# A graph layer's dense product by Strassen's scheme: seven quarter products for eight, summed in stages

## The chip, the core and the metric

The kernel runs on one NeuronCore of a Trainium2 chip. A core has five engines that issue their instructions in program order and meet at semaphores: PE (TensorE, matrix products into PSUM), DVE (VectorE), ACT (ScalarE), POOL (GpSimd) and SP, which here only starts DMA transfers. [...] The metric is the time of one execution on the device in microseconds.

## What is computed

The input `x` holds 32 batches of 512 nodes by 1024 columns, `adj` is a 512 x 512 matrix.

```
# layer 0, for each batch b
q = wq . x[b];  k = wk . x[b]                       # 1024 each
scores[m, n] = leaky_relu(q[n] + k[m], 0.01)
att = softmax(scores, axis=-1)                      # 1024 x 1024
agg = x[b] @ att.T;  y = relu(adj @ agg + bm)
x[b] = layernorm(x[b] + y)                          # over the 1024 columns
# layer 1
W = adj * adj                                       # element by element
x[b] = layernorm(x[b] + W.T @ x[b] + bias)
```

## The kernel before

**Layer 0** never forms the attention matrix. For leaky_relu the softmax weight of a pair is a product of two exponentials, one pair of them on each side of zero. So for a batch the kernel forms q and k (`pa`, `pc`, `co`, `cc`, `ro`, `rc`), finds by comparison the rank of each column among the q (`rk` on DVE) and how many q lie above the threshold of each row (`ct` on ACT), computes z = adj @ x in eight row tiles of 128 x 512 (`z`, 32 matmul calls; `zc` copies each from PSUM into the SBUF tile `zt`), scatters the rows of z in order of rank to HBM (`sc`, an indirect DMA on POOL's queue), loads them back sorted (`sl`), takes exponentials (`se`), running sums in both directions (`u`, `d`), carries across partitions (`cu`, `uc`, `cd`, `dc`), finished sums (`tu`, `td`, `te`), and writes them as a table (`tw`, `tl`). A gather (`g`, indirect DMA) fetches for each row its two table entries; `mw`, `ms`, `mx` weigh and add them, `t` transposes them on PE, `r` adds x and applies the relu, `s0` sums squares, `rt` and `rce` make the reciprocal of the deviation.

**Layer 1** is one product of a 512 x 512 matrix with the batch's 512 x 1024. `adj_2` is adj squared by element plus the identity, so the residual is inside the product. `scaled` (`w`, line 460, DVE) multiplies its four row tiles by the batch's reciprocal deviations instead of scaling x. `layer1` (`l`, line 469, PE) makes output row tile m, half h, with four matmul calls of 128 x 512 over the row tiles n; both halves share a PSUM tile of two banks. `biased` (`b`, line 480, DVE) adds the bias, held as a 128 x 1024 tile, writes the row tile `g` to SBUF and sums it; `s1` (ACT) sums squares, `r1` (POOL) makes deviation and shift, `n` (line 497, ACT) normalises in place and `st` (SP) stores. The mean of layer 0's norm is never subtracted: a constant along a row of x becomes a constant along the rows of the output, and the last norm takes that out.

**Order.** Nothing is scheduled by the machine. Three lists of words (`head`, `loop`, `tail`) are written out by hand and `emit` issues them in that order; a word such as `l.-4.2.0` is an operation, a batch relative to the loop's and its tile. Each engine gets its own instructions in the order of the list, so batches overlap: in one pass of `loop` the z of one batch, the running sums of the batch before and the layer 1 of the batch before that go by together. Waits come from data: a reader waits for its writer, and a buffer's next writer waits for its last reader. PSUM is two pools: `p1`, four tiles of one bank (tag `m`: z, carries, q and k), and `p2`, two tiles of two banks (tag `w`: transposes, layer 1). `zt`, `tab`, `got` and the scaled weights have one buffer, x has four, `g` four.

Of the kernel before, what the change touches and what calls it, by code (L numbers as in the profile page):

```python
# [24 lines left out]
F32 = mybir.dt.float32  # L26
# [7 lines left out]
P = 128  # L34
# [6 lines left out]
def adj_resnorm_kernel(  # L41
# [42 lines left out]
    rows = one.tile([P, CT, C], F32, tag="w2", name="rows")[0 : 3 * CT, 0, 0:P]  # L84
# [6 lines left out]
    bias_b = const.tile([P, N], F32, name="bias_b")  # L91
# [39 lines left out]
    adj_2 = const.tile([P, CT, C], F32, name="adj_2")  # L131

    def weights():
# [12 lines left out]
        for r in range(CT):  # L146
            a, own = adj_2[:, r, :], adj_2[:, r, r * P : (r + 1) * P]
            nc.gpsimd.tensor_tensor(a, adj_in[:, r, :], adj_in[:, r, :], ALU.mult)
            nc.gpsimd.tensor_tensor(own, own, ident, ALU.add)

# [6 lines left out]
    class Batch:  # L157
        def __init__(self):
            self.z, self.agg, self.l1, self.g = {}, {}, {}, {}
            self.w, self.v0, self.v1 = None, [], []  # L160
# [295 lines left out]
    def scaled(b, n):  # L456
        s = st[b]
        if n == 0:
            s.w2 = one.tile([P, CT, C], F32, tag="w2", name=f"w2_{b}")
        nc.vector.tensor_scalar(s.w2[:, n, :], adj_2[:, n, :], s.v0[1][:, n : n + 1], None, ALU.mult)  # L460


    def layer1(b, m, h):
        s, t = st[b], xts[b]
        if h == 0:
            s.l1[m] = p2.tile([P, N], F32, tag="w", name=f"l1_ps_{b}_{m}")
        at = slice(h * H, (h + 1) * H)
        for n in range(CT):
            nc.tensor.matmul(  # L469
                s.l1[m][:, at], s.w2[:, n, m * P : (m + 1) * P], t[:, n, at],  # L470
                start=(n == 0), stop=(n == CT - 1),
            )

    def biased(b, m):
        s = st[b]
        if not s.v1:
            s.v1 = stats(b, "1")
            s.nb = sp.tile([P, CT], F32, tag="nb", name=f"nb_{b}")
        s.g[m] = op.tile([P, N], F32, tag="g", name=f"g_{b}_{m}")
        nc.vector.scalar_tensor_tensor(  # L480
            s.g[m], s.l1[m], 1.0, bias_b, ALU.mult, ALU.add, accum_out=s.v1[0][:, m : m + 1]
        )
# [21 lines left out]
    def load_bias(b):  # L504
        nc.sync.dma_start(out=bias_b, in_=bias.partition_broadcast(P))

# [11 lines left out]
        "w": scaled, "l": layer1, "b": biased, "s1": spread1, "r1": root1, "n": norm1,  # L518
        "st": store, "bias": load_bias,
# [12 lines left out]
    ld.1 ld.2 pa.0 z.0.1 pc.0 co.0 zc.0.1 pa.1 cc.0 z.0.6 ro.0 z.0.0 rc.0 rk.0.0 ct.0.3 ct.0.4  # L532
    rk.0.3 z.0.2 ct.0.7 rk.0.2 pc.1 oq.0 ct.0.2 rk.0.5 z.0.3 zc.0.0 rk.0.1 zc.0.2 zc.0.6 rk.0.6
    rk.0.7 z.0.4 zc.0.3 ct.0.6 rk.0.4 re.0 sc.0.0 co.1 zc.0.4 z.0.5 cc.1 ct.0.5 sc.0.6 ct.0.1
    sc.0.2 sc.0.4 ro.1 zc.0.5 ct.0.0 sc.0.1 z.0.7 ce.0 sc.0.5 rc.1 we.0 sc.0.3 rk.1.3 z.1.3
    zc.0.7 ct.1.4 sc.0.7 rk.1.4 rk.1.1 z.1.0 rk.1.2 sl.0.0 rk.1.5 sl.0.1 ld.3 oq.1 rk.1.7 z.1.6
    rk.1.6 rk.1.0 se.0.0 z.1.1 ct.1.7 u.0.0 u.0.1 zc.1.3 u.0.2 se.0.1 zc.1.6 u.0.3 zc.1.0 pa.2
    u.0.4 u.0.5 z.1.7 pc.2 re.1 ct.1.5 u.0.6 u.0.7 ct.1.1 d.0.7 ct.1.2 d.0.6 z.1.4 d.0.5 zc.1.1
    ct.1.3 d.0.4 zc.1.7 d.0.3 ct.1.6 cu.0 d.0.2 pa.3 uc.0 d.0.1 zc.1.4 tu.0.0 sc.1.4 co.2 z.1.2
    pc.3 ct.1.0 cc.2 sc.1.3 tu.0.1 sc.1.6 d.0.0 sc.1.7 co.3 zc.1.2 ro.2 te.0 sc.1.2 cc.3 cd.0  # L540
    rc.2 sc.1.1 ro.3 dc.0 ce.1 ct.2.0 z.1.5 td.0.0 sc.1.0 ct.2.3 rk.2.5 tw.0.0 z.2.7 td.0.1
    zc.1.5 ct.2.1 sc.1.5 ct.2.7 rk.2.3 tw.0.1 bias.0 ct.2.5 z.2.0 tl.0 rk.2.4 ct.2.2 rk.2.7
    ct.2.6 rk.2.6 z.2.1 ct.2.4 rk.2.1 zc.2.0 zc.2.7 rk.2.0 z.2.5 rk.2.2 oq.2 rc.3 sl.1.0 sl.1.1
# [220 lines left out]
```

## Time and profile before

| | |
|---|---|
| median of 3 runs | 2082.99 us (2082.99 to 2087.58) |
| the profiled execution | 2081.17 us, its span 2079.4 us |
| PE busy | 2042.6 us, 98% |
| DVE busy | 1609.8 us, 77% |
| ACT busy | 1234.2 us, 59% |
| POOL busy | 881.8 us, 42% |
| HBM read and written | 270.80 MB and 269.29 MB, 260 GB/s |
| products of layer 1 (line 469) | 2048 instructions, 898.3 us |
| products z (line 260) | 2048 instructions, 912.4 us |

A group of the profile is read so: line of the kernel, engine, operation, output and inputs by name, shapes, count; then the busy time of the group and the mean duration of one instruction in ns; then the time that the engine stood idle just before, and what ended it. An fp32 matmul call shows as two instructions. Durations of neighbours overlap a little, so the step from one start to the next is shorter than the mean duration.

### The profile page before, as it was taken

How to read it: one execution, taken by the hardware profiler on the slowest of the kernel's cores; microseconds unless marked ns; L12 is line 12 of the kernel's file. 1: busy time of each engine (PE TensorE's matmuls, PEld its weight loads, DVE VectorE, ACT ScalarE, POOL GpSimd, SP SyncE). 2: the span in 40 equal slices, each digit the busy share in tenths (PEclk: the TensorE clock that was granted, in tenths of full speed). 3: DMA queues.
4: the chain of work that ended last, by engine and by line, in shares of the span. 5: the costliest groups of instructions: out<-in, count | busy, mean ns of one | idle time of the engine just before them, and what ended most of it. 6: DMA issues, size and time to landing. Idle time of an engine off the chain costs nothing. (4 is left out here: it accounts for less than half of the span.)

```text
span 2079.4 us, 21612 instructions
## 1 busy us (share of the span) xinstructions
PE 2042.6 (98%) x6737; PEld 1000.6 (48%) x6737; DVE 1609.8 (77%) x2700; ACT 1234.2 (59%) x2112; POOL 881.8 (42%) x1083
## 2 busy tenths in 40 slices
PE   8999999999999999999999999999999999999986
PEld 4444554445445445444445454455454445444443
DVE  4879879777788777788777887777887778777762
ACT  3646666655665556665556655557655567554554
POOL 3343454435434345344354343454443441444441
PEclk9999999999999999999999999999999999999998
DMA  4667776768676677676686666776766865676752
GB/s 187 262 268 301 272 296 266 271 261 320 235 276 238 254 299 284 243 271 236 264 324 248 265 248 251 286 299 236 279 232 257 320 254 238 228 299 269 284 213 81
DMA packets 138095, 541.53 MB, mean 260 GB/s; under 512 B 14414, under 2 KB 14426, under 8 KB 129788
## 3 DMA queue, kind: packets, MB, share of 16 engines
q1 hardware_dynamic: 80608, 337.99, 42.1%
q0 software_dynamic: 57344, 202.15, 25.5%
q8 instruction: 53, 0.87, 0.2%
q14 instruction: 62, 0.51, 0.1%
q10 hardware_dynamic: 28, 0.01, 0.0%
HBM read 270.80 MB, written 269.29 MB: 260 GB/s over the span
## 5 line engine op out<-in xcount | busy, mean ns | idle before, releaser
L260 PE MATMUL z_ps<-adj_t,x 128*128 128x512 f32 x2048 | 912.4, 595 | 3.4 <-ACT zt L266 3.4
L469 PE MATMUL l_ps<-x,w 128*128 128x512 f32 x2048 | 898.3, 595 | 8.8 <-DVE w L460 7.6
L469 PEld LDWEIGHTS l_ps<-x,w 128*128 128x128 f32 x2048 | 390.0, 191 | 500.6 <-issue 477.3
L260 PEld LDWEIGHTS z_ps<-adj_t,x 128*128 128x128 f32 x2048 | 380.4, 190 | 438.8 <-issue 428.9
L274 POOL DMA_INDIRECT sorted_z<-zt,to x256 | 356.4, 1392 | 465.7 <-ACT zt L266 304.6
L234 ACT ACTIVATE junk_s<-qb,qkc 128x1024 bf16<-128x1024 f32 x256 | 293.5, 1146 | 104.0 <-DVE qb L211 99.9
L382 POOL DMA_INDIRECT got<-table,of x256 | 275.9, 1078 | 160.8 <-issue 75.0
L221 DVE SCALAR_TENSOR_TENSOR junk_v<-qb,qkc,tie 128x1024 uint8<-128x1024 f32 x256 | 328.3, 1282 | 5.8
L404 ACT ACTIVATE got<-got,w 128x512 f32<-128x512 f32 x256 | 168.7, 712 | 238.5 <-DVE w L399 222.1
L425 POOL TENSOR_SCALAR var<-var 128x1 f32<-128x1 f32 x128 | 37.6, 294 | 535.4 <-ACT junk L418 530.8
L266 ACT COPY zt<-z_ps 128x512 f32<-128x512 f32 x256 | 146.3, 576 | 191.5 <-PE z_ps L260 188.7
L480 DVE SCALAR_TENSOR_TENSOR g<-l_ps,bias_b 128x1024 f32<-128x1024 f32 x128 | 156.2, 1221 | 92.0 <-PE l_ps L469 70.9
L409 DVE SCALAR_TENSOR_TENSOR got<-got,w 128x512 f32<-128x512 f32 x256 | 181.7, 747 | 24.1 <-ACT got L404 18.8
L418 ACT ACTIVATE junk<-g,tot 128x1024 bf16<-128x1024 f32 x128 | 146.8, 1147 | 48.4 <-DVE g L480 43.0
L322 DVE SCALAR_TENSOR_TENSOR tab<-tab,ac 128x513 f32<-128x513 f32 x224 | 168.2, 751 | 4.6
L440 DVE SCALAR_TENSOR_TENSOR x<-agg_ps,nbm,x 128x1024 f32<-128x1024 f32 x128 | 163.0, 1280 | 11.1 <-PE agg_ps L432 9.6
L497 ACT ACTIVATE g<-g,nb,var 128x1024 f32<-128x1024 f32 x128 | 158.4, 1244 | 10.6 <-POOL nb L491 10.6
L418 ACT ACTIVATE junk<-x,tot 128x1024 bf16<-128x1024 f32 x128 | 147.0, 1149 | 16.2 <-DVE x L440 11.3
L312 DVE SCALAR_TENSOR_TENSOR tab<-tab,ac 128x514 f32<-128x514 f32 x192 | 144.3, 751 | 15.3 <-ACT ac L298 12.4
L355 DVE TENSOR_TENSOR tab<-tab,carry 128x2052 f32<-128x2052 f32 x64 | 146.7, 2293 | 2.7 <-ACT carry L337 0.7
L432 PEld LDWEIGHTS agg_ps<-ident,got 128*128 128x128 f32 x1024 | 117.8, 141 | 54.2 <-issue 39.7
L432 PE MATMUL agg_ps<-ident,got 128*128 128x128 f32 x1024 | 133.0, 274 | 5.5 <-DVE g L480 2.3
(79 smaller groups left out, 1247.1 us busy)
## 6 DMA issues: line engine op xcount, KB each, us to landing
table<-tab SPq DMA_DIRECT2D x64, 2056.0 KB
tab<-sorted_z SPq DMA_DIRECT2D x64, 1028.0 KB
x<-in_x_dram SPq DMA_DIRECT2D x128, 512.0 KB
out_dram<-g SPq DMA_DIRECT2D x128, 512.0 KB
sorted_z<-zt,to POOLq DMA_INDIRECT x256
got<-table,of POOLq DMA_INDIRECT x256
adj_in<-in_adj_dram SPq DMA_DIRECT2D x1, 1024.0 KB
bias_b<-in_L_gnn_bias_dram SPq DMA_DIRECT2D x1, 512.0 KB
```

The source lines that it names most:

```text
L221: nc.vector.scalar_tensor_tensor(junk, s.qb, s.q[:, j : j + 1], tie[:, at : at + N], ALU.subtract, ALU.is_gt, accum_out=s.rank[:, j : j + 1],)
L234: nc.scalar.activation(junk, s.qb, AF.Sign, bias=s.k[:, j : j + 1], accum_out=s.sign[:, j : j + 1])
L260: nc.tensor.matmul(s.z[j], xt[:, c, j * P : (j + 1) * P], adj_t[:, c, :], start=(c == 0), stop=(c == CT - 1),)
L274: nc.gpsimd.indirect_dma_start(out=sorted_z[b % 2][:, :], out_offset=bass.IndirectOffsetOnAxis(ap=s.to[:, j : j + 1], axis=0), in_=zt[:, j ...
L322: nc.vector.scalar_tensor_tensor(v, v, c, s.zs[:, j + 1, 0:D], ALU.mult, ALU.add)
L382: nc.gpsimd.indirect_dma_start(out=s.got[:, j, :], out_offset=None, in_=table[b % 2][:, :], in_offset=bass.IndirectOffsetOnAxis(ap=s.of[:, ...
L404: nc.scalar.activation(down, down, AF.Copy, scale=s.w[:, 1, j : j + 1])
L409: nc.vector.scalar_tensor_tensor(up, up, s.w[:, 0, j : j + 1], down, ALU.mult, ALU.add)
L418: nc.scalar.activation(junk, t, AF.Square, bias=v[0][:, i : i + 1], scale=-float(N), accum_out=v[1][:, i : i + 1],)
L432: nc.tensor.transpose(s.agg[o][:, j * P : (j + 1) * P], s.got[:, j, o * P : (o + 1) * P], ident)
L440: nc.vector.scalar_tensor_tensor(t[:, o, :], s.agg[o], nbm[:, o : o + 1], t[:, o, :], ALU.max, ALU.add, accum_out=s.v0[0][:, o : o + 1],)
L469: nc.tensor.matmul(s.l1[m][:, at], s.w2[:, n, m * P : (m + 1) * P], t[:, n, at], start=(n == 0), stop=(n == CT - 1),)
```

## The change

Layer 1's product is cut into 2 x 2 quarters: the matrix into A11, A12, A21, A22 of 256 x 256, the batch into X11 to X22 of 256 x 512. Eight quarter products become seven (Winograd's form of Strassen's scheme), with

```
S1 = A21 + A22   S2 = S1 - A11   S3 = A11 - A21   S4 = A12 - S2
T1 = X12 - X11   T2 = X22 - T1   T3 = T2 - X11    T4 = T2 - X21
U  = A11 X11                      C11 = U + A12 X21
V  = U + S2 T2                    C12 = V + S1 T1 + S4 X22
Y  = V + S3 T3                    C21 = Y - A22 T4
                                  C22 = Y + S1 T1
```

- The S are made once, on POOL in `weights`. x must now be scaled before the T are formed: `norm0` (`n0`, ACT) scales its four row tiles in place, and `scaled` is gone. The T are made on DVE for each batch: T1 over X12 in place, T2 in a tile of its own, T3 and T4 in rows of `zt`.
- Each quarter product is made for two row tiles g = 0, 1 (two calls of 128 x 512 each). U, V and Y pile up in one PSUM bank (`sum`, from `p1`), and ACT copies U and then V out of it between the stages (`Uc`, `Vc`) into the row tile `g`. A12 X21 and S1 T1 (+ S4 X22) go to the two banks of `pair` (from `p2`); `Zc` copies S1 T1 out before `12` adds to it. `up` (DVE) adds pair to the copies of U and V for the upper row tiles; `lr` (DVE) adds Y to the copy of S1 T1; then `21` adds the last product onto Y and `ll` (ACT) copies it out; `ls` adds the two part sums.
- The bias comes in through PE: it is split into three bf16 parts for each half, six rows in all (`bias_parts`, once, on DVE), and a bf16 product with six rows of constants opens U (bias of the left half) and Z (difference of the halves).
- The `head`, `loop` and `tail` lists are new throughout; the loop is run for batches 11 to 24 instead of 10 to 26.

```diff
+        A21, A22 = S1, minus_A22
+        nc.gpsimd.tensor_tensor(S3, A11, A21, ALU.subtract)
+        nc.gpsimd.tensor_tensor(S1, A21, A22, ALU.add)
+        nc.gpsimd.tensor_tensor(S2, S1, A11, ALU.subtract)
+        nc.gpsimd.tensor_tensor(S4, A12, S2, ALU.subtract)
+        nc.gpsimd.tensor_scalar(minus_A22, A22, -1.0, None, ALU.mult)
...
-    def scaled(b, n):
-        s = st[b]
-        if n == 0:
-            s.w2 = one.tile([P, CT, C], F32, tag="w2", name=f"w2_{b}")
-        nc.vector.tensor_scalar(s.w2[:, n, :], adj_2[:, n, :], s.v0[1][:, n : n + 1], None, ALU.mult)
+    def norm0(b, o):
+        t = xts[b][:, o, :]
+        nc.scalar.activation(t, t, AF.Copy, scale=st[b].v0[1][:, o : o + 1])
+    def T1(b):
+        X11, X12, _, _ = quarters(b)
+        st[b].T1 = X12
+        nc.vector.tensor_tensor(X12, X12, X11, ALU.subtract)
+    def T2(b):
+        s = st[b]
+        s.T2 = one.tile([P, 2, H], F32, tag="T2", name=f"T2_{b}")
+        nc.vector.tensor_tensor(s.T2, quarters(b)[3], s.T1, ALU.subtract)
+    def T3(b):
+        st[b].T3 = zt[:, 0:2, 0:H]
+        nc.vector.tensor_tensor(st[b].T3, st[b].T2, quarters(b)[0], ALU.subtract)
+    def T4(b):
+        st[b].T4 = zt[:, 2:4, 0:H]
+        nc.vector.tensor_tensor(st[b].T4, st[b].T2, quarters(b)[2], ALU.subtract)
+    def quarter(ps, a, v, g, first=None):
+        if first is not None:
+            nc.tensor.matmul(ps, first, bias_p, start=True, stop=False)
+        for k in range(2):
             nc.tensor.matmul(
-                s.l1[m][:, at], s.w2[:, n, m * P : (m + 1) * P], t[:, n, at],
-                start=(n == 0), stop=(n == CT - 1),
+                ps, a[:, k, g * P : (g + 1) * P], v[:, k, :], start=False, stop=(k == 1),
+                skip_group_check=first is None,
             )
+    def U(b, g):
+        s = st[b]
+        s.sum[g] = p1.tile([P, C], F32, tag="m", name=f"sum_ps_{b}_{g}")
+        quarter(s.sum[g], A11, quarters(b)[0], g, first_0)
+    def U_copy(b, g):
+        rows1(b, g)
+        nc.scalar.copy(st[b].g[g][:, 0:H], st[b].sum[g])
+    def V(b, g):
+        quarter(st[b].sum[g], S2, st[b].T2, g)
+    def V_copy(b, g):
+        nc.scalar.copy(st[b].g[g][:, H:N], st[b].sum[g])
+    def Y(b, g):
+        quarter(st[b].sum[g], S3, st[b].T3, g)
...
+    def Z(b, g):
+        quarter(st[b].pair[g][:, H:N], S1, st[b].T1, g, first_10)
+    def Z_copy(b, g):
+        rows1(b, g + 2)
+        nc.scalar.copy(st[b].g[g + 2][:, H:N], st[b].pair[g][:, H:N])
+    def C12(b, g):
+        quarter(st[b].pair[g][:, H:N], S4, quarters(b)[3], g)
+    def C21(b, g):
+        quarter(st[b].sum[g], minus_A22, st[b].T4, g)
+    def upper(b, g):
+        s = st[b]
         nc.vector.scalar_tensor_tensor(
-            s.g[m], s.l1[m], 1.0, bias_b, ALU.mult, ALU.add, accum_out=s.v1[0][:, m : m + 1]
+            s.g[g], s.pair[g], 1.0, s.g[g], ALU.mult, ALU.add, accum_out=s.v1[0][:, g : g + 1]
+        )
+    def lower_right(b, g):
+        s, m = st[b], g + 2
+        nc.vector.scalar_tensor_tensor(
+            s.g[m][:, H:N], s.sum[g], 1.0, s.g[m][:, H:N], ALU.mult, ALU.add,
+            accum_out=s.part2[:, m : m + 1],
+        )
+    def lower_left(b, g):
+        s, m = st[b], g + 2
+        nc.scalar.activation(
+            s.g[m][:, 0:H], s.sum[g], AF.Copy, accum_out=s.part2[:, g : g + 1]
+        )
...
     loop = """
-    g.-3.3 rk.-1.1 ct.-1.4 g.-3.4 rk.-1.0 g.-3.6 z.-1.3 rk.-1.5 g.-3.7 b.-4.0 g.-3.5 oq.-1
-    rk.-1.6 l.-4.2.0 se.-2.0 rk.-1.4 u.-2.0 u.-2.1 l.-4.3.0 mw.-3.0 rk.-1.3 ms.-3.1 zc.-1.3
...
-    sc.-1.7 z.0.2 rc.0 g.-2.0 g.-2.2 ct.0.2 rk.0.7 g.-2.1 sl.-1.0 rk.0.2 l.-3.0.1 sl.-1.1
+    Y.-4.1 g.-3.7 up.-4.1 g.-3.5 u.-2.0 21.-4.0 re.-1 ce.-1 u.-2.1 se.-2.1 s1.-4.0 z.-1.0 u.-2.2
+    ll.-4.0 u.-2.3 r1.-4.0 lr.-4.1 mw.-3.0 21.-4.1 u.-2.4 ms.-3.0 ms.-3.3 u.-2.5 z.-1.1 oq.-1
+    ll.-4.1 ld.0 u.-2.6 zc.-1.0 mx.-3.0 ms.-3.2 u.-2.7 ms.-3.1 mx.-3.2 s1.-4.1 ls.-4.0 z.-1.3
+    ls.-4.1 mw.-3.1 n.-4.0 r1.-4.1 mx.-3.3 mx.-3.1 ms.-3.4 ms.-3.5 d.-2.7 mx.-3.4 zc.-1.1 cu.-2
+    sc.-1.0 d.-2.6 zc.-1.3 ms.-3.7 mx.-3.5 z.-1.2 ms.-3.6 sc.-1.1 mx.-3.7 n.-4.1 mx.-3.6 d.-2.5
+    s1.-4.3 st.-4.1 st.-4.0 d.-2.4 s1.-4.2 t.-3.1 r1.-4.3 d.-2.3 t.-3.3 uc.-2 r.-3.1 zc.-1.2
+    pa.0 r.-3.3 s0.-3.1 sc.-1.2 tu.-2.0 t.-3.0 r1.-4.2 pc.0 n.-4.3 t.-3.2 s0.-3.3 co.0 r.-3.2
+    z.-1.4 sc.-1.3 r.-3.0 s0.-3.2 d.-2.2 n.-4.2 cc.0 z.-1.5 d.-2.1 zc.-1.4 st.-4.2 s0.-3.0
+    st.-4.3 d.-2.0 sc.-1.4 we.-1 rt.-3 cd.-2 rce.-3 z.-1.7 dc.-2 zc.-1.5 td.-2.0 n0.-3.2 sc.-1.5
+    n0.-3.1 tu.-2.1 ro.0 tw.-2.0 n0.-3.3 z.-1.6 n0.-3.0 td.-2.1 t1.-3 U.-3.1 tw.-2.1 zc.-1.6
+    zc.-1.7 rc.0 sc.-1.7 U.-3.0 t2.-3 sc.-1.6 ct.0.1 t3.-3 11.-3.1 ct.0.6 rk.0.1 ct.0.2 Z.-3.1
+    t4.-3 Uc.-3.1 ct.0.5 11.-3.0 rk.0.4 Uc.-3.0 ct.0.3 te.-2 V.-3.1 rk.0.3 tl.-2 ct.0.0 sl.-1.0
+    sl.-1.1 rk.0.2 V.-3.0 g.-2.0 rk.0.7 Z.-3.0 Vc.-3.0 Zc.-3.1 g.-2.3 rk.0.5 ct.0.4 Y.-3.0
+    g.-2.1 rk.0.6 Zc.-3.0 ct.0.7 g.-2.2 rk.0.0 12.-3.0 se.-1.0 g.-2.4 lr.-3.0 12.-3.1 up.-3.0
+    g.-2.6 Vc.-3.1
     """
```

The last list of the tail brings the last two batches' products without any z between them:

```
t.-1.2 s0.-1.3 r1.-2.3 r.-1.2 s0.-1.0 s0.-1.2 rt.-1 n.-2.2 rce.-1 n0.-1.0 st.-2.2 st.-2.0
n0.-1.1 n0.-1.2 U.-1.1 t1.-1 s1.-2.1 U.-1.0 n0.-1.3 r1.-2.1 n.-2.3 t2.-1 11.-1.0 Uc.-1.1
```

## The prediction, on record before the changed kernel ran

> **What bounds the kernel now.** I read the page's shares first, then its groups of instructions, then windows of one loop period each, then the timeline of one period and of the end.
>
> ```profile
> span 2079.4 us, 21612 instructions
> PE 2042.6 (98%) x6737; PEld 1000.6 (48%) x6737; DVE 1609.8 (77%) x2700; ACT 1234.2 (59%) x2112; POOL 881.8 (42%) x1083
> ```
>
> TensorE (PE) is busy for all but 37 us. The windows say where it isn't. Columns: stretch and length, busy time of PE, weight load, DVE, ACT and POOL with instruction counts, granted clock, DMA share, GB/s:
>
> ```profile
> 0.00:20.00 20.00, 12.99 (x94) 7.86 (x95) 4.43 (x13) 3.41 (x5) 8.83 (x17) 1.00 0.91 349
> 944.60:1008.00 63.40, 63.40 (x213) 31.18 (x212) 50.19 (x84) 38.67 (x66) 28.08 (x34) 1.00 0.70 267
> 1008.00:1071.30 63.30, 63.30 (x212) 31.08 (x211) 50.20 (x84) 38.64 (x66) 27.96 (x34) 1.00 0.69 266
> 2020.00:2040.00 20.00, 15.28 (x54) 8.00 (x53) 14.65 (x29) 16.23 (x26) 3.26 (x9) 0.90 0.15 58
> 2060.00:2079.40 19.40, 7.43 (x18) 3.02 (x16) 2.46 (x4) 4.91 (x7) 2.00 (x6) 0.76 0.27 109
> ```
>
> A batch takes 63.33 us in the loop and PE has no gap in it; the 37 us lie at the start (7) and after 1900 us (27). DVE has 13 us free per batch, ACT 25. So PE work removed counts one for one, until another engine's chain closes the gap. The groups give the durations:
>
> ```profile
> L469 PE MATMUL l_ps<-x,w 128*128 128x512 f32 x2048 | 898.3, 595 | 8.8 <-DVE w L460 7.6
> L266 ACT COPY zt<-z_ps 128x512 f32<-128x512 f32 x256 | 146.3, 576 | 191.5 <-PE z_ps L260 188.7
> L480 DVE SCALAR_TENSOR_TENSOR g<-l_ps,bias_b 128x1024 f32<-128x1024 f32 x128 | 156.2, 1221 | 92.0 <-PE l_ps L469 70.9
> L355 DVE TENSOR_TENSOR tab<-tab,carry 128x2052 f32<-128x2052 f32 x64 | 146.7, 2293 | 2.7 <-ACT carry L337 0.7
> L497 ACT ACTIVATE g<-g,nb,var 128x1024 f32<-128x1024 f32 x128 | 158.4, 1244 | 10.6 <-POOL nb L491 10.6
> L460 DVE TENSOR_SCALAR w<-adj,var 128x512 f32<-128x512 f32 x128 | 56.5, 484 | 2.5 <-PE l_ps L469 2.1
> ```
>
> A call of a 128x512 fp32 product is two matmul instructions (2048 for 1024 calls). Their 595 ns overlap; the pitch is read from the timeline, where eight begin at 1011.70 and the next group at 1015.14: 3.44/8 = 0.43 us.
>
> [...]
>
> **The change part by part, per batch.**
> *PE.* Removed: 4 of 32 calls, 8 x 0.43 = 3.43 us. Added: four bf16 products, 4 x 0.22 = 0.88. Their bounds: 0.216 each with the weight load hidden, as now, and 0.43, an fp32 instruction. Net -2.55, bounds -2.57 and -1.7. New period 60.8. Over 32 batches -81.6 us (-54 at the dear end).
> *DVE.* Removed: four `w` (0.48) and four `g` (1.22 + 0.08): 7.1 us. Added: T1 to T4 at 1.15 = 4.6, two `up` at 1.3, two `lr` at 0.83 (L312's 0.75 plus the accumulator read), two sums at 0.17: 9.2. Now 52.3 of 60.8.
> *ACT.* Added: four `n0` like L497, 1.15 to 1.24 each, 4.8; six 512-wide copies, 3.4; two `ll` 1.5. Now 48.4 of 60.8. Both engines still fit, so what decides is order: ACT, DVE and PE issue in program order, and PE now has handoffs with ACT inside layer 1.
>
> I placed one loop period on paper with pitches from the timeline (1.27 for ACT passes with accumulator, 1.15 without, 0.63 and 0.5 for 512-wide ones, 1.33 for `rk`, 2.2 for the table additions, 0.87 for `t`, 0.17 from a matmul's last pass to its reader). Time 0 is the end of t.-3.2; PE runs without a gap:
> - U.-3.1 is due at 15.7. It needs n0.0, last of this chain on ACT: s0.2 (from 1.5), n.2, zc.4, s0.0, then `we` and `rt`, each with a 1.28 us table load (to 8.9), rce on DVE, dc, zc.5, four n0: done 14.9. Slack 0.8. Before, four `w` of 0.48 stood here.
> - V.1, due 24.9: U copy done 23.0 (behind three `ct`), T2 at 20.1 (behind two table additions, T1 and rc). Slack 1.9.
> - Y.0, due 30.3: Vc.0 29.1. Slack 1.2. 12.0, due 32.0: Zc.0 31.4, behind ct.4. Slack 0.6.
> - Y.1, due 35.5: Vc.1 is queued behind se.-1.0, which waits for the DMA of sl.-1.0. On SP that load stands behind tl.-2, which waits for te.-2 on DVE, now as late as 25.6, so it is issued at 26.1. Before:
>
> ```profile
> 1010.47 0.92 SPq L293 DMA_DIRECT2D tab<-sorted_z  x2
> ...
> 1016.78 0.30 ACT L298 ACTIVATE ac<-tab,top 128x4 f32<-128x4 f32 x1 [4.53 <-DMA tab<-sorted_z]
> ```
>
> so 6.3 us later, 32.4; ACT is there at 32.7; Vc.1 done 33.7. Slack 1.75.
> - 21.0 and 21.1, due 37.2 and 42.3: lr.0 34.4, lr.1 40.8. Slack 1.5. The next batch's zc.0, which reuses T3's rows of zt, follows.
> - From 21.1 (44.1) to the next n0.0 ACT has hardly a gap: 31 us of work beside 33 us of PE's. T3 and T4 in zt follow the scatters of those rows; the bank of z.2 (due 51.8) comes free at 51.0. The transposes (due 55.2) have their last mix at 53.6. The gathers, eight of 1.31 from 27.7, leave POOL at 38.3, before the first r1 needs it.
>
> So nothing exceeds PE, but slacks of 0.6 to 1.9 replace the wide ones of before. [...] I put 0.2 us of gap per batch, +6.4, bounds 0 and 1 (+32).
>
> *Ends.* Start: bias parts on DVE (some ten small operations, about 5 us) run before the first cc, which waits for PE anyway (it came at 17.1); five POOL operations of about 1 us come long before the first scatter. The first z now waits for all of adj_t; +1, bounds -2 and 4. Without layer 0 of a next batch, nothing hides the chain to n0: in the last batch of before PE stood for 3.9 us between transposes and `l` (2032.8 to 2036.75). Now s0 x4 (5.1), two s1 of batch -2 in the same queue (2.5), rt with its load (1.6), a norm1, rce and two n0 follow: some 13 us after the first transpose, PE filling about 3: 10 of standing, +6. Batch -2 is alike: before 2.8, now about 8 (`we` and `rt` both load, then two n0, against 4 us of transposes and carries), +5. Against that, three whole layer-1 products instead of two and a bit now stand behind the last z and cover the last batch's scatter, table and gather: -2. Sum +9, bounds 0 and 18. After the last product: ll, s1, r1, n, store, some 12 us as before.
>
> **Sum**: 2079.4 - 81.6 + 6.4 + 1 + 9 = 2014 for the span. The profiled run took 2081.17 with its 2079.4, so 1.8 lie around it: 2016. The median of the runs, 2082.99, is 1.8 above that run and they repeat within 0.3%: I leave 2016.
>
> **The rivals.**
> (1) *The ring through ACT and DVE becomes the bound.* Chain: 21.1, ACT's stretch to rt, rce, dc, DVE's stretch td.0 to lr.1 (31 us), 21.1 again: by my pitches 59.5 us, 1.3 below PE. For: DVE would be 86% busy, both stretches lack gaps, and the T operations in this form are unseen. Against: every row's duration is steady (rk 1266 to 1286 ns). With 4% more it is 62 us: 1.2 above PE's 60.8 over 28 batches, 34 in place of the 6 put in, so 2044 us.
> (2) *All slacks hold and the end is as good as before*: 2079.4 - 82 + 1.8 = 1999. For: the loop of before has no gap although four engines hand over in it. Against: the chain of n0 in the last two batches.
> (3) *The bf16 products cost an fp32 instruction each*: +27, so 2043. [...]
> (4) *Slower than before: the load of the sorted sums.* If sl.-1.0 lands late, ACT stands at se.-1.0, Vc.1 behind it stands, and PE stands at Y.1 in every batch. For: tl, before it on SP, now comes late, so the load starts closer to its reader. ACT waited 177 us in all for this DMA before, up to 11.6 at once, where nothing urgent was queued behind. PE stands once landing takes more than 6.3 + 0.3 + 1.75 = 8.35 us; the forecast's gain is (2083 - 2016)/28 = 2.4 per batch, so from 10.75 us on the kernel is slower; at 11.5 it is 28 x 0.75 = 21 above 2083: 2104. Against: the DMA engines carry about what they carry now at that place, the gathers and this load.
> That the change does not do what it says is out: the instruction lists show 28 fp32 and 4 bf16 products per batch.
>
> **How the numbers follow.** Forecast 0.62; (1) 0.14; (2) 0.10; (3) 0.07; (4) 0.05; no change 0.02 (a mixture that ends within 0.3%, what a measurement of this kernel can tell from no change). Faster 0.93, same 0.02, slower 0.05. Range: from (2), 1998, up to where (1) and (3) lie, 2046; above that are (4) and the far end of (1).
>
> **What would show it.** Right: loop period 60.8 to 61.2 with PE full; 1792 fp32 layer-1 instructions in place of 2048 and 128 bf16 ones at a pitch near 0.22; idle of PE in the loop under 0.4 us per batch, mostly ahead of 12.0 and U. Wrong: PE waits on `n0`, the Z copy or `lr` of over 1 us per batch (1); ACT's wait for tab<-sorted_z with PE idle before Y.1 (4); bf16 pitch over 0.3 (3); idle after 1880 us much over 36.

## The result, and the profile after

The changed kernel takes 2070.64 us (median of 4 runs, 2069.47 to 2071.41) where the kernel before, beside it on the same chip, takes 2084.6 us: a ratio of 0.9931, with a 95% interval from 0.9914 to 0.9948. It is faster by 0.7%, which is 14 us, where 67 were forecast. 2070.6 also lies above the range (1998 to 2046). The profiled execution has a span of 2068.1 us at a mean granted TensorE clock of 0.989; before it was 2079.4 us at 0.994.

The page's first lines, span and busy time of each engine:

```profile
span 2068.1 us, 22068 instructions
PE 2005.4 (97%) x6609; PEld 958.9 (46%) x6609; DVE 1686.9 (82%) x2778; ACT 1494.8 (72%) x2560; POOL 848.7 (41%) x1088
```

PE's busy time fell by 37 us only, and its idle time rose from 36.8 to 62.7 us. The windows of the changed kernel answer to those shown of before (same columns: stretch and length, PE, weight load, DVE, ACT, POOL, granted clock, DMA share, GB/s):

```profile
0.00:20.00 20.00, 12.83 (x66) 7.40 (x66) 13.82 (x24) 2.45 (x3) 15.88 (x22) 1.00 0.85 325
943.90:1005.80 61.90, 61.90 (x207) 29.73 (x206) 52.43 (x87) 46.82 (x81) 25.93 (x33) 1.00 0.69 272
1005.80:1067.70 61.90, 61.90 (x207) 29.74 (x206) 52.45 (x87) 46.83 (x81) 25.93 (x33) 1.00 0.69 273
...
2010.00:2030.00 20.00, 13.57 (x52) 7.58 (x53) 11.89 (x23) 17.30 (x28) 3.50 (x9) 0.87 0.13 50
2048.70:2068.10 19.40, 7.08 (x16) 2.57 (x14) 3.48 (x8) 10.85 (x16) 4.01 (x12) 0.77 0.27 109
```

In the loop PE is full, as before, and a batch takes 61.90 us instead of 63.33. So the loop saves 1.43 us per batch, not the forecast 2.55. The groups of the changed kernel:

```profile
L508 ACT ACTIVATE x<-x,var 128x1024 f32<-128x1024 f32 x128 | 138.3, 1146 | 1.4 <-DVE var L504 1.3
L540 PE MATMUL sum_ps<-x,adj 128*128 128x512 f32 x256 | 132.7, 642 | 18.9 <-ACT x L508 18.9
L529 DVE TENSOR_TENSOR zt<-T,x 128x1024 f32<-128x1024 f32 x32 | 39.2, 1224 | 0.8
L538 PE MATMUL sum_ps<-bias_p,first 6*128 6x512 bf16 x64 | 24.9, 389 | 0.0
L538 PEld LDWEIGHTS <-first 6*128 6x128 bf16 x128 | 11.6, 91 | 96.8 <-issue 96.8
```

L508 is `norm0`, L529 is `T3`, L538 the bias product, L540 a quarter product. Two things stand out. L540's first group, the products that follow a bias product, carries 18.9 us of idle time ahead of it, all ended by `norm0`. And the weight loads of L538 have 96.8 us of idle time ahead of them, ended by nothing that the profile shows: 0.76 us for each of 128, where the timeline below shows 0.24 ahead of the load of a z product.

Where PE idles, from windows of both kernels (us):

| stretch | before | after |
|---|---|---|
| 0 to 700 us | 9.9 | 24.2 |
| 700 to 1700 us | 0 | 0 |
| 1700 us to the end | 26.9 | 38.5 |

The start of the first `residual` of a batch, read from DVE's timeline, shows the progress (us):

| batch | before | after |
|---|---|---|
| 4 | 351.3 | 355.2 |
| 5 | 411.7 | 417.4 |
| 6 | 472.6 | 487.0 |
| 8 | 598.8 | 614.8 |
| 25 | 1675.4 | 1666.4 |
| end of the span | 2079.4 | 2068.1 |

The changed kernel comes to batch 8 16.0 us late, gains 25.0 us over the next 17 batches and only another 2.3 us over the last six and the end: 11.3 us in all. The orders of the two kernels differ, so work taken ahead differs at a landmark too; the idle times above are free of that.

So there are three questions: why the loop saves 1.43 us per batch, what the head loses, and what the end loses.

### The profile page after: what moved, and what is told of

It reads as the page before. It is cut to its first block, busy times and chain, and to the rows that moved or that the text cites. A ratio compares the mean times of both kernels' runs of the same rounds, so it can differ in the third digit from the quotient of the medians.

```text
span 2068.1 us, 22068 instructions
## 1 busy us (share of the span) xinstructions
PE 2005.4 (97%) x6609; PEld 958.9 (46%) x6609; DVE 1686.9 (82%) x2778; ACT 1494.8 (72%) x2560; POOL 848.7 (41%) x1088
## 4 chain that ended last, share of the span: by engine, by line
PE 71%; DMA 7%; DVE 6%; POOL 3%; ACT 2%; issue 2%; SPq 0%; ACTq 0%; DVEq 0%; POOLq 0%
PE z_ps L310 30%; PE sum_ps L540 16%; PE pair_ps L540 8%; DMA got<-table,of 5%; PE agg_ps L482 5%; PE pair_ps L575 4%; POOL got L432 3%; PE qk_ps L221 2%; DMA table<-end 1%; DVE got L459 1%; PE carry_ps_False L380 1%; DVE tab L405 1%; PE q_tp L252 1%; PE carry_ps_True L380 1%; PE sum_ps L538 1%
## 5 line engine op out<-in xcount | busy, mean ns | idle before, releaser
L324 POOL DMA_INDIRECT sorted_z<-zt,to x256 | 327.0, 1277 | 423.7 <-ACT zt L316 323.1
L432 POOL DMA_INDIRECT got<-table,of x256 | 268.8, 1050 | 331.9 <-DVE junk_v L271 117.3
L475 POOL TENSOR_SCALAR var<-var 128x1 f32<-128x1 f32 x128 | 63.4, 496 | 427.0 <-ACT junk L468 411.8
L468 ACT ACTIVATE junk<-x,tot 128x1024 bf16<-128x1024 f32 x128 | 146.8, 1147 | 18.9 <-DVE x L490 18.0
L540 PE MATMUL sum_ps<-x,adj 128*128 128x512 f32 x256 | 132.7, 642 | 18.9 <-ACT x L508 18.9
L508 ACT ACTIVATE x<-x,var 128x1024 f32<-128x1024 f32 x128 | 138.3, 1146 | 1.4 <-DVE var L504 1.3
L405 DVE TENSOR_TENSOR tab<-tab 128x1539 f32<-128x1539 f32 (+1 forms) x64 | 129.4, 2025 | 0.8 <-ACT tab L387 0.7
```

The source lines that it names most:

```text
L324: nc.gpsimd.indirect_dma_start(out=sorted_z[b % 2][:, :], out_offset=bass.IndirectOffsetOnAxis(ap=s.to[:, j : j + 1], axis=0), in_=zt[:, j ...
L405: nc.vector.tensor_tensor(v, v, c, ALU.add)
L432: nc.gpsimd.indirect_dma_start(out=s.got[:, j, :], out_offset=None, in_=table[b % 2][:, :], in_offset=bass.IndirectOffsetOnAxis(ap=s.of[:, ...
L468: nc.scalar.activation(junk, t, AF.Square, bias=v[0][:, i : i + 1], scale=-float(N), accum_out=v[1][:, i : i + 1],)
L540: nc.tensor.matmul(ps, a[:, k, g * P : (g + 1) * P], v[:, k, :], start=False, stop=(k == 1), skip_group_check=first is None,)
```

## Experiments on the bias product

**Leaving it out.** The quarter product that followed a bias product starts the sum itself. This leaves the bias out of the result; the rest is as in the changed kernel.

```
-        if first is not None:
-            nc.tensor.matmul(ps, first, bias_p, start=True, stop=False)
...
-                ps, a[:, k, g * P : (g + 1) * P], v[:, k, :], start=False, stop=(k == 1),
+                ps, a[:, k, g * P : (g + 1) * P], v[:, k, :],
+                start=(first is not None and k == 0), stop=(k == 1),
```

> Leaves out the bias products (the bias of this case is zero). Theory A, the bias products are what the loop lost: each takes 0.52 us of PE (0.32 from its start to the next, 0.10 before it, 0.10 behind its successor), so the period falls from 61.90 by 4 x 0.52 to 59.8, PE without gaps, some 20 to 32 batches long: 2005 to 2030 us. Rival, the ring through ACT and DVE is close behind: the period stops near 60.5 to 61.5 with PE waiting on the n0 scaling, the Z copy or lr in every batch; 2040 to 2060 us.

Measured: 2047.52 us (2043.63 to 2050.88), ratio to before 0.9838 (0.9821 to 0.9856). From the first `U` of a batch to that of the next, read where PE had no gap (999.70 to 1059.54 us), it takes 59.84 us. The difference to 61.90 is four bias products: (61.90 - 59.84)/4 = 0.515 us each, where the forecast took 0.22 and set 0.43 as the dear bound. The period is theory A's; the total lies in the rival's range, because at 59.84 us PE's gaps are back (11.7 us between 700 and 1700 us) and the mean distance of the residuals of batches 8 to 25 is 60.6 us. The ring that the rival names is not what ends them, though. Eight of the nine gaps (8.8 us) end with ACT's copy of a z out of PSUM. The copy stands behind mixes on ACT, the mixes wait for their weights from DVE, and DVE waits for a gather to land (one of the eight, on DVE, ACT and PE):

```profile
972.28 0.17 DVE L445 TENSOR_TENSOR w<-bd,got 128x8 f32<-128x8 f32 x1 [3.91 <-DMA got<-table,of]
...
973.10 1.34 ACT L454 ACTIVATE got<-got,w 128x512 f32<-128x512 f32 x2 [2.79 <-DVE w L449]
...
974.96 1.55 PE L310 MATMUL z_ps<-adj_t,x 128*128 128x512 f32 x3 [1.60 <-ACT zt L316]
```

In these 1000 us DVE waits 1.5 to 4.1 us for a gather in each batch, in the changed kernel 0.9 at most.

**More rows.** The six rows of parts and constants stay, the other 122 rows are zero, so that the bias product has 128 rows like its neighbours. The result is the same.

```
-    bias_p = const.tile([6, H], BF16, name="bias_p")
-    first_0 = const.tile([6, P], BF16, name="first_0")
-    first_10 = const.tile([6, P], BF16, name="first_10")
+    bias_p = const.tile([P, H], BF16, name="bias_p")
+    first_0 = const.tile([P, P], BF16, name="first_0")
+    first_10 = const.tile([P, P], BF16, name="first_10")
+    for t in (bias_p, first_0, first_10):
+        nc.vector.memset(t, 0.0)
```

> The bf16 bias products get 128 rows in place of 6 (zeros in the rest). If a bf16 product between fp32 ones cannot hide its weight load nor that of its successor: unchanged, 0.52 us each, period 61.9. If the six rows are what hinders the early load: near 0.22 each, period 60.7.

Measured in a single run: 2052.63 us, period 60.71. Four more runs gave an interval:

> The kernel with 128-row bias products once more, for an interval: 2050 to 2055, that is 0.7 to 0.9% under the changed kernel; if the single time seen before was an accident, over 2060.

Measured: 2054.13 us (2051.26 to 2063.69), ratio to before 0.9882 (0.9848 to 0.9915); the changed kernel had 0.9931 (0.9914 to 0.9948). The two intervals just touch; the period is what tells the kernels apart. A product with more than twenty times the rows is cheaper: (60.71 - 59.84)/4 = 0.218 us. PE's and the weight loads' timelines say why. The changed kernel, PE first (start, duration, engine, line, operation):

```profile
1003.45 2.31 PE L310 MATMUL z_ps<-adj_t,x 128*128 128x512 f32 x5
1005.69 0.39 PE L538 MATMUL sum_ps<-bias_p,first 6*128 6x512 bf16 x1
1006.01 1.98 PE L540 MATMUL sum_ps<-x,adj 128*128 128x512 f32 x4
1007.92 0.38 PE L538 MATMUL sum_ps<-bias_p,first 6*128 6x512 bf16 x1
```

and its weight loads:

```profile
1004.74 0.19 PEld L310 LDWEIGHTS z_ps<-adj_t,x 128*128 128x128 f32 x1 [0.24 <-issue]
1005.69 0.09 PEld L538 LDWEIGHTS <-first 6*128 6x128 bf16 x1 [0.76 <-issue]
1006.01 0.30 PEld L540 LDWEIGHTS sum_ps<-x,adj 128*128 128x128 f32 x2 [0.23 <-issue]
```

The kernel with 128 rows, PE:

```profile
1001.27 0.38 PE L540 MATMUL sum_ps<-bias_p,first 128*128 128x512 bf16 x1
1001.49 1.88 PE L542 MATMUL sum_ps<-x,adj 128*128 128x512 f32 x4
1003.21 0.38 PE L540 MATMUL sum_ps<-bias_p,first 128*128 128x512 bf16 x1
```

and its weight loads:

```profile
1000.85 0.10 PEld L540 LDWEIGHTS <-first 128*128 128x128 bf16 x1 [0.24 <-issue]
1001.28 0.41 PEld L542 LDWEIGHTS sum_ps<-x,adj 128*128 128x128 f32 x2 [0.33 <-issue]
1001.92 0.19 PEld L542 LDWEIGHTS sum_ps<-x,adj 128*128 128x128 f32 x1 [0.24 <-issue]
```

With 128 rows the load of the bias product starts at 1000.85, 0.42 us ahead of its product at 1001.27: it is hidden. With six rows it starts at 1005.69, with its own product, and the next product's load at 1006.01 likewise. From one bias product to the next it is 1007.92 - 1005.69 = 2.23 us against 1003.21 - 1001.27 = 1.94; the four quarter-product instructions account for 4 x 0.43 = 1.72 of each. The weight loads that come into the open are some 0.1 us ahead of the product and 0.1 to 0.2 behind it.

**The type.** To tell the rows from the type, the six-row products were made fp32. Six rows of the identity stand in for the constants, and of the bias, which is zero in the inputs, only the first half is taken and read twice; so a product with zeros is added, and not the bias by parts.

```
-    bias_p = const.tile([6, H], BF16, name="bias_p")
-    first_0 = const.tile([6, P], BF16, name="first_0")
-    first_10 = const.tile([6, P], BF16, name="first_10")
+    bias_p = const.tile([6, Q], F32, name="bias_p")
+    first_0 = first_10 = ident[0:6, :]
...
-            nc.tensor.matmul(ps, first, bias_p, start=True, stop=False)
+            both = bias_p.rearrange("p (o c) -> p o c", o=1).broadcast_to([6, 2, Q])
+            nc.tensor.matmul(ps, first, both, start=True, stop=False)
```

> The bias products in fp32, still six rows (rows of the identity stand for the constants, so the zero bias goes to other rows). If the change of type is what exposes the loads: two instructions at 0.43 with hidden loads, 0.86 each, period 61.9 - 2.08 + 3.44 = 63.3. If the six rows expose them: 0.86 plus 0.2 to 0.3 each, period 64.1 to 64.5.

Measured in a single run: 2155.54 us, period 64.84. A six-row fp32 product costs (64.84 - 59.84)/4 = 1.25 us, where two instructions at the pitch of 0.43 are 0.86. That is 0.39 over them, more than the 0.2 to 0.3 of the second theory and far from the first. Four steps from start to start are 0.53 us in place of 0.43: the one into the product, its own two, and the first of its successor. PE's timeline of this kernel shows 1.05 us from its start to the next one's:

```profile
1036.77 1.12 PE L535 MATMUL sum_ps<-bias_p,ident 6*128 6x512 f32 x2
1037.82 1.98 PE L537 MATMUL sum_ps<-x,adj 128*128 128x512 f32 x4
```

So the exposed loads come with the rows, in either type. That a bf16 product among fp32 ones might cost a change of type has fallen: with 128 rows the same bf16 product costs 0.218.

**All four in one place.** If each stretch of six-row products exposes one load at its beginning and one at its end, four in a row should pay once.

```
+    def open_sums(b, g):    # both sums and both pairs opened at the first U or C11 of a batch
+        for i in (g, 1 - g):
+            nc.tensor.matmul(s.sum[i], first_0, bias_p, start=True, stop=False)
+        for i in (g, 1 - g):
+            nc.tensor.matmul(s.pair[i][:, H:N], first_10, bias_p, start=True, stop=False)
```

> The four bias products of a batch one after the other, ahead of its first U. If the exposed loads come only where bf16 meets fp32: 0.2 + 4 x 0.22 + 0.1 = 1.2 in place of 2.08 per batch, period 61.0, and 0.9 x 20 to 32 batches off the time: 2042 to 2053 us. If each bf16 load is exposed by itself: 4 x 0.32 + 0.2 = 1.5, period 61.3, 2052 to 2059 us. Opening the sums of both row tiles so early could make PE wait for their banks: then gaps ahead of the first bias product.

Measured: 2092.9 us (2091.43 to 2094.73), ratio to before 1.0059 (1.0043 to 1.0076): slower than both kernels. PE's timeline:

```profile
1016.50 0.60 PE L552 MATMUL sum_ps<-bias_p,first 6*128 6x512 bf16 x2
1016.94 0.37 PE L554 MATMUL pair_ps<-bias_p,first 6*128 6x512 bf16 x1
1018.31 0.37 PE L554 MATMUL pair_ps<-bias_p,first 6*128 6x512 bf16 x1 [0.99 <-DVE qb L261]
```

and the weight loads of the row:

```profile
1016.50 0.11 PEld L552 LDWEIGHTS <-first 6*128 6x128 bf16 x2 [0.76 <-issue]
1016.73 0.31 PEld L554 LDWEIGHTS <-first 6*128 6x128 bf16 x2
```

Within the row a product costs no more than one of 128 rows: 0.44 us for the first two together, and the loads of the later ones are ahead of their products (the third's at 1016.73 for 1016.94). The first load still starts with its own product, and from the fourth's start to the next start it is 0.30 us. So what is paid for is the change between six rows and 128, at both ends of a stretch. But opening the second pair that early needs a PSUM bank that `rc` of another batch still reads: 0.99 us of waiting, more than was saved. The residuals of batches 8 to 25 come every 62.7 us.

**How many rows.** Left open was what in the six rows does it. These three have the loop's order in the head (next section), so they stand beside the run there with six rows (2057.4) and the one with 128 (2036.7). The edit is the second one above with 32, 64 or 96 in place of `P`.

> Bias products of 32 rows (six of parts or constants, the rest zero), with the loop's order from round 7 on: beside the run with 128 rows and that order (2036.7, period 60.7, start to start 0.215 us). Theory W: a weight load is hidden only if it takes the whole array, so 32 rows show their own load and the next one's as six did: 0.52 us a product, period 61.9, about 2057. Rival S: only the odd number of six is at fault; 0.22 us, period 60.7, 2037.

> The same with 64 rows. Theory W: 0.52 us a product, period 61.9, about 2057. Rival S, or a boundary between 32 and 64: 0.22 us, 60.7, 2037.

> The same with 96 rows. If what counts is whether the array is addressed as a whole, 96 rows go as 128 do or as 64 do, and not between: 0.22 us with 60.7 and 2037, or 0.52 us with 61.9 and 2057. If the exposed load shrinks with the rows left out, between.

Measured, one run each: 32 rows 2059.65 us with a period of 61.9, 64 rows 2057.96 with 61.9, 96 rows 2039.22 with 60.7. PE's timeline with 64 rows, then with 96:

```profile
1008.86 0.39 PE L540 MATMUL pair_ps<-bias_p,first 64*128 64x512 bf16 x1
1009.18 1.98 PE L542 MATMUL pair_ps<-x,adj 128*128 128x512 f32 x4
```

```profile
1048.39 0.38 PE L540 MATMUL sum_ps<-bias_p,first 96*128 96x512 bf16 x1
1048.61 1.88 PE L542 MATMUL sum_ps<-x,adj 128*128 128x512 f32 x4
```

0.32 us to the next start with 64 rows, as with six, and 0.22 with 96, as with 128. The cost doesn't shrink with the rows left out; it steps somewhere between 64 and 96. As it was worded, theory W falls too: 96 rows are not all 128, and their step is the 0.22 us of a product with hidden loads. The weight loads of the kernel with 64 rows, around the product at 1008.86:

```profile
1007.91 0.19 PEld L542 LDWEIGHTS sum_ps<-T,S 128*128 128x128 f32 x1 [0.24 <-issue]
1008.86 0.09 PEld L540 LDWEIGHTS <-first 64*128 64x128 bf16 x1 [0.76 <-issue]
1009.18 0.30 PEld L542 LDWEIGHTS pair_ps<-x,adj 128*128 128x128 f32 x2 [0.23 <-issue]
```

So, in these runs, a load of 128 rows between products of 128 starts ahead of its product (1000.85 for 1001.27), and one of six rows between products of six likewise (1016.73 for 1016.94). Where 128 rows change to 6, 32 or 64 or back, the load starts with its product: at 1005.69 and 1006.01 with six rows, at 1009.06 and 1009.38 with 32 (products at 1009.07 and 1009.38), at 1008.86 and 1009.18 with 64. What the hardware does inside was not tested.

## Experiments on the head

In the changed kernel PE's longest gap between 100 and 700 us is this one (PE's timeline):

```profile
482.98 0.66 PE L482 MATMUL agg_ps<-ident,got 128*128 128x128 f32 x2 [3.79 <-issue]
484.26 1.13 PE L482 MATMUL agg_ps<-ident,got 128*128 128x128 f32 x3 [0.62 <-DVE got L459]
```

These are the transposes of batch 6. They wait for mixes, these for gathers, and these for the last table row. SP's queue shows that row's write (L425, `tl`) behind a load of sorted sums (L343) that stood until 451.14, and POOL's timeline the gather behind it:

```profile
451.14 0.38 SPq L343 DMA_DIRECT2D tab<-sorted_z  x1
451.57 0.35 SPq L425 DMA_DIRECT2D table<-end  x1
```

```profile
456.91 0.97 POOL L432 DMA_INDIRECT got<-table,of  x1 [11.17 <-DMA table<-end]
```

**That write earlier.** `te` and `tl` go right behind a batch's second `tu`, in all three lists.

```
-    ... te.3 ct.5.5 rk.5.5 tl.3 U.2.1 sl.4.0 ...
+    ... tu.3.1 te.3 tl.3 ...
```

> The changed kernel, with the 2 KB write of a batch's last table row (tl) and the copy before it (te) named right behind the batch's second table_up in every list, ahead of the sums loads of the next batch; nothing else is changed. Theory L: the head's extra 16 us of TensorE idle come from that write standing behind a load that waits for the next batch's scatters, so that gathers, mixes and transposes are late. Then the longest head gap (3.8 us ahead of the transposes at 483 us) shrinks to under 1 us, POOL's waits for the table fall from 74 us, and the time is 2061 to 2066. Rival R: the head is held by the work of VectorE and ScalarE themselves; the write comes earlier, the gap stays over 3 us, and the time is 2069 to 2072.

> The same move of the last table row's write on top of the kernel whose bias products have 128 rows. Theory L: its longest head gap (5.8 us at 485 us) closes, 2043 to 2048. Rival R: the gap stays, 2051 to 2054.

Measured: 2097.74 us (ratio to before 1.0075, 1.0051 to 1.0099), and with 128 rows 2126.96 us (1.0211, 1.0184 to 1.0238). Both are slower than before, and neither theory had said so. The gap at 483 us is gone, as theory L had it, but 2.7 us open ahead of the last product of the batch before it, at 472, and the residuals of batches 5 and 6 stay 69.9 us apart (69.6 in the changed kernel). In the loop PE now idles 11 us between 700 and 1700 us. The list of waits of this kernel has ACT's wait for the sorted sums and POOL's wait for the table:

```profile
ACT ac L348 <- DMA tab<-sorted_z: 159.6, 39, 8.3
POOL got L432 <- DMA table<-tab: 133.6, 17, 13.5
```

(us in total, times, longest). In the changed kernel the first is 45.6 us, and the second doesn't appear. So this move only shifts the waits. It doesn't settle what the write's place costs the head, for two reasons. The edit was made in all three lists, and most of the 27 us were lost behind the head: batch 8 comes at 619.5 us against 614.8 in the changed kernel. And it puts the write ahead of the table's other writes (`tw`) too, where the loop's list, tried next, has it behind them and ahead of the load only.

**The loop's order in the head.** The lists of head and loop hold the same kinds of work. From round 7 of the head on (where Y.3.1 stands) the words were written in the order of the loop's list; at that point the written head is 10 words ahead of the loop's order and 2 behind.

```
-    head = """ ... (rounds 7 to 10 as written for the head)
+    head = """ ... (the same words up to Y.3.1, then each round as `loop` has it)
```

> The changed kernel; from round 7 of the head on (that is from Y.3.1, some 320 us in) the instructions go in the order of the loop's list instead of the order written for the head; the set of instructions is the same, and so is everything before and behind. Theory H: the 16 us that the head lost (the residual of batch 8 starts at 614.8 us against 598.8 before) are made by the order written for those rounds; in the loop's order the distance of the residuals of batches 5 and 6 falls from 69.6 to 62 to 64 us, batch 8 comes at 604 to 608, and the time is 2059 to 2064. Rival D: in these rounds VectorE, ScalarE and GpSimd are still behind from the start-up, whatever the order; the distances stay within 2 us of theirs, and the time is 2067 to 2073.

Measured: 2057.4 us (2055.64 to 2061.22), ratio to before 0.9873 (0.9856 to 0.9889), where the changed kernel had 0.9931 (0.9914 to 0.9948). The residuals of batches 5 and 6 are 61.9 us apart, batch 8 starts at 606.1; distance and time are a little better than theory H had them. Windows of this kernel:

```profile
300.00:500.00 200.00, 198.65 (x691) 96.06 (x690) 169.19 (x274) 156.98 (x265) 87.04 (x108) 1.00 0.68 269
500.00:700.00 200.00, 200.00 (x653) 94.82 (x652) 171.38 (x277) 149.60 (x256) 80.14 (x103) 1.00 0.70 276
```

PE idles 1.4 us in these 400 us, where it idled 8.3 in the changed kernel, and the granted clock of the first stretch is 1.00 where it was 0.98. Theory H holds: DVE and ACT do more in the same time (169.2 against 161.3 and 157.0 against 145.1 us in the first stretch), so they were not behind, they were waiting. Part of the gain may be the write of the last row after all: in the loop's order it goes out ahead of the load, and the first gather of batch 6 comes at 451.25 us instead of 456.91 (SP's queue, then POOL):

```profile
449.32 0.24 SPq L425 DMA_DIRECT2D table<-end  x1
451.11 0.92 SPq L343 DMA_DIRECT2D tab<-sorted_z  x2
```

```profile
451.25 1.54 POOL L432 DMA_INDIRECT got<-table,of  x1 [6.66 <-DVE junk_v L271]
```

No run moves the write ahead of the load and nothing else, so how much the rest of the order brings is open.

**From round 5 on.**

> The same from round 5 on (from Y.1.1, some 210 us in), where the written head is 53 instructions ahead of the loop's list. Theory H: as in the run beside it or 1 to 3 us better, 2057 to 2063. Rival D: work that the written head has taken ahead is done later here and is missed; batch 8 later than 615, the time 2072 or more.

Measured: 2070.97 us (ratio to before 0.9942, 0.9926 to 0.9959): no better than the changed kernel. Batch 8 comes at 617.2. The distances from batch 3 on are 61.9 each, but between 100 and 300 us PE idles 15.2 us (8.7 in the changed kernel). That is rival D's reading, with batch 8 later than 615 us as it said, though the time is 1 us short of its 2072: in these rounds the written head's 52 words of work taken ahead are worth as much as the loop's order brings later.

**Both gains together.**

> 128-row bias products and the loop's order from round 7 on. If both gains hold and add up: 2041 to 2046. If the head is held by other engines than TensorE (rival D), as with the 128 rows alone: 2051 to 2056.

Measured: 2036.71 us (2033.53 to 2039.93), ratio to before 0.9777 (0.9759 to 0.9795). This version beats both kernels, the one before by 2.2%, and is below the 2041 to 2046 that adding the two gains had given. The medians fall by 13 us with the order alone, by 17 with the rows alone and by 34 with both. With the written head the rows had brought less than they could: PE idled 34.0 us before 700 us with the rows alone (24.2 in the changed kernel), the gap above grew to 5.8 us, and batch 8 came no earlier (617.6). With both, PE idles 20.9 us before 700 us and batch 8 comes at 597.9.

## Experiments on the end

The changed kernel's longest gap (PE's timeline) and what ACT does meanwhile (ACT's timeline):

```profile
1978.56 0.39 PE L538 MATMUL sum_ps<-bias_p,first 6*128 6x512 bf16 x1
1988.49 3.78 PE L540 MATMUL sum_ps<-x,adj 128*128 128x512 f32 x4 [9.54 <-ACT x L508]
```

```profile
1982.82 1.15 ACT L468 ACTIVATE junk<-x,tot 128x1024 bf16<-128x1024 f32 x1
...
1984.27 1.28 ACT L500 ACT_TABLE_LOAD   x1
1985.57 0.30 ACT L500 ACTIVATE var<-var,eps 128x4 f32<-128x4 f32 x1
1986.25 4.26 ACT L508 ACTIVATE x<-x,var 128x1024 f32<-128x1024 f32 x4 [0.39 <-DVE var L504]
```

**A shorter chain.** For the last two batches the inverse root goes to POOL (`pow`) and two of four scalings to DVE.

```
     def root0(b):
+            if b >= B - 2:
+                root(v, slice(0, CT))
+                return
...
     def norm0(b, o):
+        if b >= B - 2 and o in (1, 3):
+            nc.vector.tensor_scalar(t, t, st[b].v0[1][:, o : o + 1], None, ALU.mult)
```

> 128-row bias products, and in the last two batches the first norm's inverse root on GpSimd with pow instead of ScalarE's root (a table load of 1.28 us and a VectorE reciprocal less), and two of its four scalings on VectorE. Theory N: the two long tail gaps (10.0 and 6.0 us ahead of the first product of the last two batches) are the chain root, table load, four scalings of 1.15 us on ScalarE. They fall to about 6.5 and 3 us, the time to 2044 to 2048. Rival M: the gaps are set by the mixes and transposes before them; they fall by under 1 us each and the time stays at 2050 to 2054.

Measured: 2055.66 us (ratio to before 0.9875, 0.9852 to 0.9899), against 2054.13 for the same kernel without the edit: no gain. The two gaps are 10.5 and 6.3 us, where they were 10.0 and 6.0 to 6.2. That they did not shrink doesn't decide between the theories, since the edit made the chain no shorter. POOL's timeline of this kernel:

```profile
1969.24 2.31 POOL L477 TENSOR_SCALAR var<-var 128x4 f32<-128x4 f32 x1 [7.78 <-ACT junk L470]
1971.64 1.47 POOL L478 TENSOR_TENSOR var<-var,power 128x4 f32<-128x4 f32 x1
```

The two small operations on POOL take 3.9 us from start to end, in place of a table load, a root and a reciprocal that took 2.0 (1984.27 to 1986.25 above), and outweigh the one scaling of 1.1 us that the first product waits for less. In the changed kernel the second of them, L476 there, works on 128x1 elements in the second norm. It takes 2.61 us at 1971.54, beside DVE's addition of 1539 elements (1.75 us from 1971.99), and 0.55 at 2019.24, beside the `residual`, which reads one operand from PSUM. No run took the addition away, so that it is the cause is not shown.

**The loop's order to the end.** The last eleven rounds in the loop's order, words beyond the last batch left out.

> The kernel of the run before (128-row bias products, the loop's order from round 7 of the head on), and the last eleven rounds too in the loop's order, with what lies beyond the last batch left out. Theory T: the end's idle time (some 35 us of TensorE from 1900 us on) is made by the order written for the tail, as in the head: 2024 to 2031. Rival E: in the last batches the chain gathers, mixes, transposes, norm, products has no other batch's work beside it, whatever the order; the time stays at 2034 to 2041, or is longer by what the written tail had gained by taking work ahead, up to 2060.

Measured: 2047.49 us (2046.28 to 2050.02), ratio to before 0.9831 (0.9815 to 0.9848), some 11 us longer than the kernel it was made from (2036.71, 0.9777). The residual of batch 29 comes earlier (1880.5 against 1889.0 us), but those of the last two come 55.7 and 52.5 us after the one before, instead of 53.3 and 42.6. Rival E holds: the written tail takes work ahead, and that is worth more than the loop's order. PE still stands 9.6 us before the last batch's first product.

## Why the prediction was wrong

The sign, the direction of each loop step and the engine that bounds were right; the size was not. By its own steps:

- **The bias product** failed: "four bf16 products, 4 x 0.22", with 0.43 as the dear bound. It measured 0.515. Both bounds took the weight load as hidden; the sentence "with the weight load hidden, as now" is where it went wrong, since the loads that the trace of before shows hidden around products all have 128 rows. That trace has no bf16 product, so the 0.22 was not shown either. The trace of after shows the sign that the forecast had set for a dear product, a pitch over 0.3: 0.32. 32 x 4 x (0.515 - 0.22) = 38 us. With 128 rows the product measured 0.218 us.
- **Removed work** was right: without any bias product the period is 59.84, and 63.33 - 3.43 is 59.90. With 128 rows it is 60.71, where 60.8 was forecast.
- **DVE 52.3, ACT 48.4 per batch** were right, ACT within 1.6 us: 52.4 and 46.8. The T operations take 1.22 us.
- **Handoffs of 0.6 to 1.9 us of slack, 0.2 us of gap per batch** did not come up: PE has no gap between 700 and 1700 us, so the 6.4 us that the forecast put in weren't spent. But each batch had 1.1 us more of room than the forecast's 60.8 would have left. At that period, with 128 rows, PE idles 3.4 us in the same 1000 us, which is the 0.2 us per batch, though not at the places that were named: as with 59.84 us, the gaps over 0.3 us end with a z copy that stands behind mixes and a gather. The step had followed the gathers only until they leave POOL, not until they land.
- **The start, +1 (bounds -2 and 4)** failed: PE idles 14.4 us more before 700 us. The step counted only what the setup adds before the first scatter; the new order list of the head was not followed to batch 7, although each of its rounds can lose what the placed loop round was shown not to. Of the 14.4, 6.9 lie between 300 and 700 us and go with the order from round 7 on; those before 300 us stay unexplained. The forecast had also read PE's 37 us of idle time before as 7 at the start and 27 after 1900 us; the other 3 lay in the head too, between 100 and 500 us.
- **The end, +9 (0 to 18)** was near: 11.6 us more idle. The chain to `norm0` stands 9.5 us for the last batch but one (forecast 8) and 5.9 for the last (forecast 10), and smaller gaps before them make up the rest. Not foreseen was the clock.
- **The clock** was not in the sum: the mean granted clock fell from 0.994 to 0.989, which spread evenly over 2005 us of busy PE would be some 10 us, an estimate. That PE is slow behind a gap can be read above: the four instructions behind the longest one take 3.78 us (1988.49), where four take 1.98 in the loop (1006.01). No run changed the clock alone.

The sum, from PE's busy and idle time. Busy: the forecast had 2042.6 - 81.6 = 1961.0, measured are 2005.4. The bias product makes 38 of these 44 us, the work removed gives 2 back, and some 8 are left, near the estimate for the clock but not shown to be it. Idle: the forecast had 36.8 + 6.4 + 1 + 9 = 53.2, measured are 62.7: 6.4 less in the loop, 13.4 more at the start, 2.6 more at the end. The terms of start and end are differences of two single executions and good to a few us. Mending the bias product and the head together doesn't bring the forecast's time: 2036.7 is still 21 us above 2016, and in that execution PE idles 67.6 us, 43 of them after 1700 us.

The rivals. (3), the dear bf16 product, was nearest in kind, for another reason than the one it named, and beyond its bound. (1), the ring through ACT and DVE, was put at 59.5 us; at a period of 61.9 it isn't seen, and at 59.84 PE's gaps end with the z copies behind a gather and not with the operations that it named. (4) is out: ACT's waits for the sorted sums fell from 177.0 to 45.6 us in all, the longest from 11.6 to 7.0. (2) was right about the slacks and wrong about the rest.

## What to carry to other kernels

A small product put between large ones is not priced by its size: here one of six rows cost 0.515 us and one of 128 rows 0.218. See in a trace whether its weight load and its successor's are hidden, and if they aren't, try filling its rows with zeros, which here made a product with more rows cost 0.3 us less. Work taken off the engine that bounds is not all won: with the rows filled PE had some 35 us less to do, waited 17.5 us longer, and the kernel won 17. Where the order of work is written out by hand, the steady loop that one has reasoned through is only one of three lists: a head that differs from it for no reason of the start-up can lose what the loop gains, and running the loop's order there is a cheap test. A gap that has a visible last releaser need not close when that one thing is moved: here the write that came last, moved alone in every list, cost some 27 us.

## What the hardware showed that was not expected

- A 512-column product of 6, 32 or 64 rows between 128-row products costs 0.515 us in the loop (bf16), one of 96 or 128 rows 0.22. In fp32 six rows cost 1.25 us. Six-row bf16 products in a row start 0.22 us apart: the cost lies at the change of rows.
- The same POOL operation on 128x1 elements (L476 of the changed kernel) took 2.61 us beside a DVE addition of 1.75 us and 0.55 us beside a DVE instruction that reads PSUM, in one execution.
- A stretch with gaps in PE's work showed a lower granted clock: from 300 to 500 us it was 0.98 in the changed kernel, where PE idled 6.9 us, and 1.00 with the loop's order in the head, where it idled 1.4.
